# One PSUM bank for two convolution tiles: projections of 256 columns, with the causal tail carried from half to half

## The chip, the cores and the metric

The kernel runs on one core of a Trainium2 chip. Its time is the device time of one execution in microseconds. The core has five engines with instruction queues of their own: TensorE (PE in the profile, its weight loads PEld), VectorE (DVE), ScalarE (ACT), GpSimd (POOL) and SyncE (SP), which here only starts transfers. Matmuls write to PSUM, eight banks of 512 float32 values on each of 128 partitions. Everything here is float32.

## The reference, cut to what matters

The block is a Mamba-2 mixer and a linear layer with sign weights, each behind a modulated layer norm, over 4 sequences of 512 tokens with 512 channels:

```
h    = layernorm(x) * (1 + ca) + sa
proj = h @ in_proj_w.T                   # 2048 channels x|B|C, 1024 z, 64 dt
y    = causal depthwise conv1d(x|B|C, 4 taps)      # pads 3 zeros at the sequence's start
xBC  = silu(y + conv_bias)
...                                      # chunked scan over 128 tokens: decays, C.B, states
out  = ((y_ssm + D * x / dt) * silu(z + z_bias)) @ out_proj_w.T
x    = x + ga * out
x    = x + gb * (sign(W) * mean|W| applied to layernorm(x) * (1 + cb) + sb, + bias)
```

What the change touches is the convolution: output token t takes the projected values of tokens t-3 to t. A token at the start of a stretch needs the three tokens before it.

## The kernel before

The 2048 tokens are worked on in 8 halves of 256 tokens (`T`), two to a sequence (`HPB`); the even half begins a sequence, the odd one continues it. A half has 2 chunks of 128 tokens, and a chunk has 4 units (a group pair `gp` each); so there are 64 units.

**Front of a half.** `f_hT` turns the normed input into `hT`, channels on partitions, with 3 more columns in front: zeros for an even half (a GpSimd memset, L339), the last three columns of the half before for an odd one (a GpSimd copy, L341). `f_dt` makes the step sizes (`pa`, then a series on VectorE). `proj` (L431) multiplies one tile of 128 channels: 4 products over the input channels, which the chip runs as 8 matmul instructions, over all 259 columns for the convolution, over the last 256 for z. So the convolution's values for the three tokens before a half are projected a second time.

`conv_pair` (L436) works on two tiles of 128 channels. Each tile has a PSUM tile `pm` of its own (profile names pp_B, pp_C, pp_x) of 259 columns. ScalarE evicts tap 3 with the bias into `u` (L446), VectorE adds taps 0 to 2 out of PSUM (three multiply-adds, L450), ScalarE takes the tanh of the pair, and VectorE makes the silu (L455). There are 8 pairs in a half: two of B, two of C, four of x. `f_z` does the same for z without a convolution, with two tiles of 256 columns in one PSUM tile (pp_z). `f_Bt` and `f_xt` turn B and x back to tokens on TensorE (pt_bt, pt_xt), and ScalarE copies them out (xpad for x, L489). `f_turned_sums` makes `pn` and `st`.

**PSUM.** `gy` has two banks, `py` one, and all other PSUM tiles share the tag "mm" with five buffers of one bank each:

```python
ps = ctx.enter_context(tc.tile_pool(name="ps", bufs=5, space=PSUM))
```

**A unit.** `stage0` and `stage1` load the running sums, broadcast over partitions, into two of four decay buffers (SyncE's queue), take 16 exponentials of 128x128 on ScalarE (L545), and multiply by C.B on VectorE (L623). `burst` makes the products C.B and C times state (`gy`). `stage2` makes the output `py` in two strips of 16 matmul instructions each (32 columns of the array each, glued together), adds and gates with z on VectorE and GpSimd (L664 to L673), and makes the new state: xd on GpSimd (L680), pst on TensorE (L685), S. `tail1` to `tail3` make the output projection po (L722), the second norm and the linear layer pf (L758) of a chunk.

**Order.** The loop at the end goes through steps, one a unit. In each step, the front's pieces of this step are emitted first, then the burst, `stage2` of the step's unit, and `stage0` and `stage1` of the unit two steps on. The lists FIRST and SECOND (halves 0 and 1) and FRONT (all others) say which piece belongs to which step. FRONT's begin in the half before: step 3 hT and dt, step 4 a B and a C pair, step 5 two x pairs, pn and a turn of B, step 6 a B and a C pair and two turns of x, step 7 two x pairs, steps 8 to 10 z. Half 1 has its first B pair in step 2. Within this, the Tile framework's scheduler orders each engine's instructions when the kernel is built, by program order and by what its cost model takes to be ready; it also gives out the buffers and sets all waits. `tc.issue_after(ins)` keeps instructions of the same engine behind `ins`. Before the change, it holds the first of the py strips for units 4 to 7 alone, behind the last projection of half 1; `behind` does it for turns.

Of the kernel before, what the change touches and what calls it, by code (L numbers as in the profile page):

```python
# [39 lines left out]
def adaln_mamba_block(  # L40
# [26 lines left out]
    keep = ctx.enter_context(tc.tile_pool(name="keep", bufs=1))  # L67
    dram = ctx.enter_context(tc.tile_pool(name="dram", bufs=1, space=bass.MemoryType.DRAM))
    ps = ctx.enter_context(tc.tile_pool(name="ps", bufs=5, space=PSUM))
    wk = ctx.enter_context(tc.tile_pool(name="wk", bufs=2))  # L70
# [43 lines left out]
    win = keep.tile([P, NK, PROJ], F32, name="win")  # L114
# [44 lines left out]
    cw = keep.tile([P, NCONV // P, KS], F32, name="cw")  # L159
    nc.sync.dma_start(cw, conv_w)  # L160
    cb = keep.tile([P, NCONV // P], F32, name="cb")
# [142 lines left out]
    H = [dict(B={}, C={}, xt={}, xs={}, bt={}, z={}) for _ in range(NHALF)]  # L304
# [28 lines left out]

    def f_hT(h, turned=None):
        b = h // HPB

        hT = wk.tile([P, NK, KS - 1 + T], F32, tag="hT", name=f"hT_{h}")
        if h % HPB == 0:
            nc.gpsimd.memset(hT[:, :, 0 : KS - 1], 0.0)  # L339
        else:  # L340
            nc.gpsimd.tensor_copy(hT[:, :, 0 : KS - 1], H[h - 1]["hT"][:, :, T:])  # L341
        for d2 in range(NK // 2):
            pt = turned[d2] if turned else turned_x(h, d2)
            for q in range(2):
                dt = 2 * d2 + q
                nc.scalar.activation(
                    hT[:, dt, KS - 1 :], pt[:, q, :], AF.Identity,
                    bias=modT[:, 0, dt, b : b + 1], scale=modT[:, 1, dt, b : b + 1],
                )
        H[h]["hT"] = hT  # L350

    def f_dt(h):

        hT = H[h]["hT"]

        queue = nc.sync if h == 0 else nc.gpsimd

        def small(tag, bufs=1):
            return wk.tile([P, CH], F32, tag=tag, name=f"{tag}_{h}", bufs=bufs)

        pa = ps.tile([P, CH], F32, tag="mm", name=f"pa_{h}")
        for k in range(NK):
            for c in range(2):
                mm(pa[c * NH : (c + 1) * NH, :], win[:, k, NCONV + DI :],  # L367
                   hT[:, k, KS - 1 + c * CH : KS - 1 + (c + 1) * CH], start=(k == 0), stop=(k == NK - 1))
        u, r, q, dt, relu = (small(n) for n in ("du", "dr", "dq", "da", "dl"))
        nc.vector.tensor_scalar(relu, pa, 0.0, None, ALU.max)  # L370
        nc.scalar.activation(u, pa, AF.Abs)
        nc.scalar.activation(u, u, AF.Exp, scale=-1.0)
        nc.vector.tensor_scalar(r, u, 2.0, None, ALU.add)
        nc.vector.reciprocal(r, r)
        nc.vector.tensor_mul(u, u, r)
        nc.vector.tensor_mul(q, u, u)
        nc.vector.tensor_scalar(dt, q, SERIES[0], None, ALU.mult)
        for cf in SERIES[1:]:
            nc.vector.scalar_tensor_tensor(dt, dt, cf, q, ALU.add, ALU.mult)
        nc.vector.scalar_tensor_tensor(dt, dt, 1.0, u, ALU.add, ALU.mult)  # L380
        nc.vector.scalar_tensor_tensor(dt, dt, 2.0, relu, ALU.mult, ALU.add)

        up = relu
        nc.vector.tensor_tensor_scan(up, ones, dt, 0.0, ALU.mult, ALU.add)
        sh = small("sh", 2)
        nc.vector.tensor_scalar(sh, up, up[:, CH // 2 - 1 : CH // 2], None, ALU.subtract)
        with tc.issue_after(last_win):
            queue.dma_start(sums_d[h].rearrange("c h s -> (c h) s"), sh)
        es = small("es", 2)
        nc.scalar.activation(es, up, AF.Exp, scale=-1.0)  # L390
        with tc.issue_after(last_win):
            queue.dma_start(e_d[h].rearrange("c h s -> (c h) s"), es)

        ntot = wk.tile([P, 1], F32, tag="ntot", name=f"ntot_{h}", bufs=1)
        nc.vector.tensor_scalar(ntot, up[:, CH - 1 : CH], -1.0, None, ALU.mult)
        ed = u
        nc.scalar.activation(ed, up, AF.Exp, bias=ntot)

        dg = q
        nc.vector.tensor_scalar(dg, ident, es[:, CH - 1 : CH], None, ALU.mult)  # L400

        nc.vector.reciprocal(r, dt)
        nc.vector.tensor_scalar(r, r, dsk, None, ALU.mult)
        with tc.issue_after(last_win):
            for c in range(2):
                queue.dma_start(r_d[h, :, c, :], r[c * NH : (c + 1) * NH, :])
        H[h].update(turn=(sh, ed, dg))
# [20 lines left out]
            st=st[:, 0:P], ed=st[:, P : 2 * P], dec=st[:, 2 * P :].rearrange("p (j h) -> p j h", h=HPG)  # L428
        )

    def proj(pm, h, col, lo):  # L431
        for k in range(NK):
            last = mm(pm, win[:, k, col : col + P], H[h]["hT"][:, k, lo:], start=(k == 0), stop=(k == NK - 1))  # L433
        return last.ins

    def conv_pair(h, t0, name, dst=None):  # L436

        u = wk.tile([P, 2, T], F32, tag="u", name=f"u_{name}_{h}", bufs=4)
        for j in range(2):
            t = t0 + j
            pm = ps.tile([P, KS - 1 + T], F32, tag="mm", name=f"pp_{name}{j}_{h}")
            H[h]["last"] = proj(pm, h, t * P, 0)
            nc.scalar.activation(  # L446
                u[:, j, :], pm[:, KS - 1 :], AF.Identity, bias=cb[:, t : t + 1], scale=cw[:, t, KS - 1 : KS]
            )
            for k in range(KS - 1):
                nc.vector.scalar_tensor_tensor(  # L450
                    u[:, j, :], pm[:, k : k + T], cw[:, t, k : k + 1], u[:, j, :], ALU.mult, ALU.add
                )
        th = wk.tile([P, 2, T], F32, tag="th", name=f"th_{name}_{h}")
        nc.scalar.activation(th, u, AF.Tanh)
        nc.vector.scalar_tensor_tensor(u if dst is None else dst, th, 1.0, u, ALU.add, ALU.mult)  # L455
        return u
# [49 lines left out]
    def f_z(h, j):  # L506
        pm = ps.tile([P, 2, T], F32, tag="mm", name=f"pp_z{j}_{h}")
        for q in range(2):
            H[h]["last"] = proj(pm[:, q, :], h, NCONV + (2 * j + q) * P, KS - 1)
        u = wk.tile([P, 2, T], F32, tag="u", name=f"uz_{h}_{j}", bufs=4)  # L510
        for q in range(2):
            nc.scalar.activation(  # L512
                u[:, q, :], pm[:, q, :], AF.Identity, bias=zb[:, 2 * j + q : 2 * j + q + 1], scale=0.5
            )
        th = wk.tile([P, 2, T], F32, tag="th", name=f"thz_{h}_{j}")
        nc.scalar.activation(th, u, AF.Tanh)
        z = wk.tile([P, 2, T], F32, tag="z", name=f"z_{h}_{j}", bufs=6)
        nc.vector.scalar_tensor_tensor(z, th, 1.0, u, ALU.add, ALU.mult)
        H[h]["z"][j] = z
# [108 lines left out]
    def stage2(h, c, gp):  # L628
# [4 lines left out]
        n = f"{h}_{c}_{gp}"  # L633
        k = (h % HPB) * 2 + c
# [12 lines left out]
        for r in range(2):  # L647
            glued([
                partial(
                    mm, py[32 * j : 32 * j + 32, r, :],  # L650
                    xp[:, r * 2 * P + 32 * (2 * j + q) : r * 2 * P + 32 * (2 * j + q) + 32],
                    ets[r][:, 2 * j + q, :], start=(q == 0), stop=(q == 1),
                )
                for q in range(2) for j in range(HPG // 2)
            ], H[1]["last"] if (h, c) == (0, 1) else None)

        cs = slice(c * CH, (c + 1) * CH)
        zg = H[h]["z"][gp][:, :, cs]
# [1 line left out]
        t = wk.tile([P, 2, CH], F32, tag="gm", name=f"yt_{n}", bufs=3)  # L660
# [14 lines left out]
        if k < HPB * 2 - 1:  # L675
# [8 lines left out]
            for r in range(2):  # L684
                mm(pst[r * NS : (r + 1) * NS, :], bt[:, r * NS : (r + 1) * NS], xd2[:, r * P : (r + 1) * P],  # L685
                   start=True, stop=True)
# [77 lines left out]
    def behind(h, f, *args):  # L764
# [9 lines left out]
        (7, f_x, (2,)), (7, behind, (f_Bt, 1)), (7, f_x, (3,)),  # L774
        (8, f_z, (0,)), (8, behind, (f_xt, 2)), (8, f_z, (1,)), (8, behind, (f_xt, 3)),
        (9, f_z, (2,)), (10, f_z, (3,)),
    ]

# [15 lines left out]
    NU = 2 * NP  # L794
    steps = {}

    def at(step, f, *args):
        steps.setdefault(step, []).append((f, args))

    for h in range(NHALF):  # L800
        for step, f, args in (FIRST, SECOND)[h] if h < 2 else FRONT:
            at(max(0, h - 1) * NU + step, f, h, *args)
        if h % HPB == 0:
            at(h * NU + 3, load_gates, h // HPB)
        if h == 0:
            at(0, load_late, h)
            at(1, behind, 0, late_mods)
            at(2, load_wout)
            for o in range(NK):
                at(o // 2 + 2, signs, o)  # L810
# [12 lines left out]
    h = NHALF - 1  # L823
# [65 lines left out]
```

## Time and profile before

| | |
|---|---|
| time, three runs | 748.45 us median (746.47 to 752.62) |
| profiled execution | 747.6 us, of which the span of the profile is 745.9 us |
| mean granted clock of TensorE | 0.991 |
| busy: TensorE, VectorE, ScalarE, GpSimd | 711.2, 602.6, 523.7, 260.4 us |
| matmuls of the convolution (pp_x, pp_B, pp_C) | 512, 256, 256 of 259 columns |
| matmuls of z | 512 of 256 columns |

Busy time counts an engine's instructions from start to end, and matmuls overlap; so the spacing of matmuls in the chain or the timeline says more of their cost than their mean duration. A wait is put down to the instruction that came last among those waited for, as far as the profile tells. A wait of TensorE for an instruction of ScalarE or VectorE can be for data or for a PSUM bank that this instruction was the last to read.

### The profile page before, as it was taken

Reading aid. Unit: us, or ns where it says so; the run is one execution under the profiler, and the core shown is the slowest. Engines: PE = TensorE matmul, PEld = TensorE weight load, DVE = VectorE, ACT = ScalarE, POOL = GpSimd, SP = SyncE. Lnnn points to the kernel's source line nnn. Section 1 sums busy time; section 2 is a strip of 40 time slices with the busy share of each in tenths; the row PEclk is TensorE's granted clock in tenths of the full one; section 3 lists DMA queues with packets and bytes.
Section 4 is the critical chain, followed back from the end, with each engine's and each line's share of the span. In section 5 each row is a group of like instructions: output and inputs, shape, how many; then the busy total and the mean of one; then the engine's idle time right before and its main releaser. Section 6 shows DMA issues by size and latency. Waiting matters only on the chain.

```text
span 745.9 us, 15107 instructions
## 1 busy us (share of the span) xinstructions
PE 711.2 (95%) x5196; PEld 503.2 (67%) x5196; DVE 602.6 (81%) x1218; ACT 523.7 (70%) x1507; POOL 260.4 (35%) x313
## 2 busy tenths in 40 slices
PE   6999979899999999999999999999999999999997
PEld 3787647566677666686667666876667866677654
DVE  3968889866999579986899769996699867997795
ACT  2476668648796596775877777764969658798941
POOL 4021325334242433353224243533324232343452
PEclk9999989899999999999999999999999999999999
DMA  8991865435654266434634246543544436458610
GB/s 280 317 289 39 237 164 121 113 86 138 125 146 125 63 158 140 106 101 99 158 101 119 75 108 165 149 110 69 139 125 121 129 79 175 104 152 167 143 58 28
DMA packets 119068, 99.25 MB, mean 133 GB/s; under 512 B 73984, under 2 KB 97152, under 8 KB 118992
## 3 DMA queue, kind: packets, MB, share of 16 engines
q1 hardware_dynamic: 117808, 96.39, 50.6%
q0 software_dynamic: 896, 1.38, 0.6%
q8 instruction: 41, 0.67, 0.4%
q10 hardware_dynamic: 288, 0.52, 0.2%
q14 instruction: 35, 0.29, 0.1%
HBM read 92.47 MB, written 5.79 MB: 132 GB/s over the span
## 4 chain that ended last, share of the span: by engine, by line
PE 77%; ACT 14%; DVE 5%; issue 2%; DMA 2%; ACTq 0%; POOL 0%; SPq 0%; DVEq 0%
PE pp_x L433 16%; PE po L722 15%; PE pp_z L433 12%; ACT decay L545 10%; PE pp_B L433 7%; PE pp_C L433 7%; PE pf L758 4%; PE py L211 3%; PE py L214 3%; PE gy L211 2%; PE pt_xt L463 2%; PE pst L685 2%; PE pa L367 1%; DMA decay<-sums_d 1%; ACT h L742 1%
## 5 line engine op out<-in xcount | busy, mean ns | idle before, releaser
L545 ACT ACTIVATE decay<-decay,st 128x128 f32<-128x128 f32 x960 | 293.0, 395 | 4.0 <-DMA decay<-sums_d 3.7
L623 DVE SCALAR_TENSOR_TENSOR decay<-decay,gm 128x1024 f32<-128x1024 f32 x120 | 156.8, 1308 | 25.1 <-ACT decay L545 24.1
L433 PE MATMUL pp_x<-hT,win 128*128 128x259 f32 x512 | 122.5, 394 | 5.8 <-ACT decay L545 5.8
L433 PE MATMUL pp_z<-hT,win 128*128 128x256 f32 x512 | 118.1, 383 | 0.0
L433 PEld LDWEIGHTS pp_x<-hT,win 128*128 128x128 f32 x512 | 98.0, 195 | 24.1 <-ACT decay L545 6.0
L722 PE MATMUL po<-wout,z 128*128 128x512 f32 x256 | 113.9, 595 | 0.0
L433 PEld LDWEIGHTS pp_z<-hT,win 128*128 128x128 f32 x512 | 94.3, 189 | 16.1 <-issue 3.3
L680 POOL TENSOR_TENSOR xd<-xpad,st 128x256 f32<-128x256 f32 x48 | 37.6, 784 | 188.3 <-PE pst L685 143.0
L450 DVE SCALAR_TENSOR_TENSOR u_x<-pp_x,cw,u_x 128x256 f32<-128x256 f32 x192 | 82.9, 473 | 1.4 <-ACT u_x L446 0.5
L722 PEld LDWEIGHTS po<-wout,z 128*128 128x128 f32 x256 | 47.4, 190 | 52.6 <-issue 51.7
L512 ACT ACTIVATE uz<-pp_z,zb 128x256 f32<-128x256 f32 x64 | 26.8, 468 | 62.3 <-PE pp_z L433 62.3
L670 POOL TENSOR_TENSOR yt<-yt,xs 128x256 f32<-128x256 f32 x46 | 41.1, 893 | 84.4 <-DVE yt L669 84.4
L214 PE MATMUL py<-decay,xpad 128*32 128x128 f32 x1680 | 67.4, 276 | 0.0
L673 POOL TENSOR_TENSOR z<-yt,z 128x256 f32<-128x256 f32 x62 | 58.5, 944 | 17.1 <-DVE yt L672 13.6
L433 PE MATMUL pp_B<-hT,win 128*128 128x259 f32 x256 | 60.9, 388 | 0.9 <-ACT st L426 0.9
L758 PE MATMUL pf<-bwT,h 128*128 128x512 f32 (+1 forms) x136 | 59.1, 575 | 0.8 <-ACT h L742 0.6
L433 PE MATMUL pp_C<-hT,win 128*128 128x259 f32 x256 | 59.0, 382 | 0.0
L503 POOL TENSOR_TENSOR xs<-u_x,rr 128x512 f32<-128x512 f32 x32 | 42.1, 1318 | 40.8 <-DVE u_x L455 40.8
L433 PEld LDWEIGHTS pp_B<-hT,win 128*128 128x128 f32 x256 | 47.0, 189 | 10.8 <-ACT st L426 1.7
L433 PEld LDWEIGHTS pp_C<-hT,win 128*128 128x128 f32 x256 | 47.8, 189 | 7.8 <-DVE u_B L450 0.3
L446 ACT ACTIVATE u_x<-pp_x,cb,cw 128x256 f32<-128x256 f32 x64 | 35.2, 559 | 25.1 <-PE pp_x L433 24.8
L211 PE MATMUL py<-decay,xpad 128*32 128x128 f32 x240 | 47.5, 280 | 3.8 <-ACT decay L545 2.8
(155 smaller groups left out, 1134.0 us busy)
## 6 DMA issues: line engine op xcount, KB each, us to landing
decay<-sums_d SPq DMA_DIRECT2D x120, 256.0 KB
decay<-sums_d SPq DMA_DIRECT2D x120, 128.0 KB
rr<-r_d SPq DMA_DIRECT2D x64, 128.0 KB
e<-e_d SPq DMA_DIRECT2D x96, 64.0 KB
win<-in_w_inT SPq DMA_DIRECT2D x4, 1024.0 KB
xr<-in_x SPq DMA_DIRECT2D x16, 256.0 KB
res<-o SPq DMA_DIRECT2D x15, 256.0 KB
x<-in_x SPq DMA_DIRECT2D x14, 256.0 KB
```

Source lines behind the costliest of these rows:

```text
L211: first = products[0]()
L214: product()
L433: last = mm(pm, win[:, k, col : col + P], H[h]["hT"][:, k, lo:], start=(k == 0), stop=(k == NK - 1))
L450: nc.vector.scalar_tensor_tensor(u[:, j, :], pm[:, k : k + T], cw[:, t, k : k + 1], u[:, j, :], ALU.mult, ALU.add)
L503: nc.gpsimd.tensor_tensor(xs, xc, rr, ALU.mult)
L545: nc.scalar.activation(ets[r][:, i, :], ets[r][:, i, :], AF.Exp, bias=H[h]["st"][:, hd : hd + 1], scale=-1.0)
L623: nc.vector.scalar_tensor_tensor(ets[r], ets[r], 1.0, bc_mid(gm[:, r, :], HPG), ALU.min, ALU.mult)
L670: ew.tensor_add(t, t, xs)
L673: ew.tensor_mul(zg, t, zg)
L680: nc.gpsimd.tensor_tensor(xd, xg, by_head(H[h]["ed"][:, hd0 : hd0 + HPP]), ALU.mult)
L722: last_po = mm(po, H[h]["z"][g // 2][:, g % 2, c * CH : (c + 1) * CH], wout[:, g, :], start=(g == 0), stop=(g == NKI - 1))
L758: mm(pf, h2[:, k, :], bwT[:, k, cols], start=(k == 0), stop=(k == NK - 1))
```

## The change

`hT` has 256 columns and none in front, and both memset and copy on GpSimd go. A convolution pair's two tiles share one PSUM tile of 2x256 columns, one bank. All projections of the pair are emitted before its evictions. In an even half, ScalarE copies the pair's last three projected columns to `ctail`. `f_carry`, five GpSimd operations in an odd half, makes from `ctail` what taps 0 to 2 of the half before add to the first three tokens; VectorE adds this `carry` to `u`, and the multiply-adds then run over 253 to 255 columns. Where a sequence begins, nothing is added, which is the zero padding. The first py strip of every unit is kept behind the last projection emitted so far (`newest["proj"]`).

```diff
     def f_hT(h, turned=None):
         b = h // HPB
-
-        hT = wk.tile([P, NK, KS - 1 + T], F32, tag="hT", name=f"hT_{h}")
-        if h % HPB == 0:
-            nc.gpsimd.memset(hT[:, :, 0 : KS - 1], 0.0)
-        else:
-            nc.gpsimd.tensor_copy(hT[:, :, 0 : KS - 1], H[h - 1]["hT"][:, :, T:])
+        hT = wk.tile([P, NK, T], F32, tag="hT", name=f"hT_{h}")
...
-    def proj(pm, h, col, lo):
+    def proj(pm, h, col):
         for k in range(NK):
-            last = mm(pm, win[:, k, col : col + P], H[h]["hT"][:, k, lo:], start=(k == 0), stop=(k == NK - 1))
+            last = mm(pm, win[:, k, col : col + P], H[h]["hT"][:, k, :], start=(k == 0), stop=(k == NK - 1))
+        newest["proj"] = last.ins
         return last.ins
...
+    ctail = keep.tile([P, NCONV // P, KS - 1], F32, name="ctail")
+    carry = keep.tile([P, NCONV // P, KS - 1], F32, name="carry")
+    ctmp = keep.tile([P, NCONV // P, KS - 1], F32, name="ctmp")
+
+    def f_carry(h):
+        for k in range(KS - 1):
+            n = KS - 1 - k
+            to = carry if k == 0 else ctmp
+            nc.gpsimd.tensor_tensor(to[:, :, 0:n], ctail[:, :, k:], bc(cw[:, :, k], n), ALU.mult)
+            if k > 0:
+                nc.gpsimd.tensor_add(carry[:, :, 0:n], carry[:, :, 0:n], ctmp[:, :, 0:n])
+
     def conv_pair(h, t0, name, dst=None):
...
+        both = slice(t0, t0 + 2)
         u = wk.tile([P, 2, T], F32, tag="u", name=f"u_{name}_{h}", bufs=4)
+        pm = ps.tile([P, 2, T], F32, tag="mm", name=f"pp_{name}_{h}")
+        for j in range(2):
+            H[h]["last"] = proj(pm[:, j, :], h, (t0 + j) * P)
         for j in range(2):
             t = t0 + j
-            pm = ps.tile([P, KS - 1 + T], F32, tag="mm", name=f"pp_{name}{j}_{h}")
-            H[h]["last"] = proj(pm, h, t * P, 0)
             nc.scalar.activation(
-                u[:, j, :], pm[:, KS - 1 :], AF.Identity, bias=cb[:, t : t + 1], scale=cw[:, t, KS - 1 : KS]
+                u[:, j, :], pm[:, j, :], AF.Identity, bias=cb[:, t : t + 1], scale=cw[:, t, KS - 1 : KS]
             )
+        if h % HPB < HPB - 1:
+            nc.scalar.copy(ctail[:, both, :], pm[:, :, T - KS + 1 :])
+        if h % HPB:
+            nc.vector.tensor_add(u[:, :, 0 : KS - 1], u[:, :, 0 : KS - 1], carry[:, both, :])
+        for j in range(2):
+            t = t0 + j
             for k in range(KS - 1):
+
+                past = KS - 1 - k
+                uk = u[:, j, past:]
                 nc.vector.scalar_tensor_tensor(
-                    u[:, j, :], pm[:, k : k + T], cw[:, t, k : k + 1], u[:, j, :], ALU.mult, ALU.add
+                    uk, pm[:, j, 0 : T - past], cw[:, t, k : k + 1], uk, ALU.mult, ALU.add
                 )
...
-            ], H[1]["last"] if (h, c) == (0, 1) else None)
+            ], newest["proj"])
...
+    for h in range(1, NHALF, 2):
+        at((h - 1) * NU + 2, f_carry, h)
```

More of the change, by code (lines that the diff above doesn't have):

```diff
@@ L346, in f_hT @@
                 nc.scalar.activation(
-                    hT[:, dt, KS - 1 :], pt[:, q, :], AF.Identity,
+                    hT[:, dt, :], pt[:, q, :], AF.Identity,
                     bias=modT[:, 0, dt, b : b + 1], scale=modT[:, 1, dt, b : b + 1],
@@ L367, in f_dt @@
                 mm(pa[c * NH : (c + 1) * NH, :], win[:, k, NCONV + DI :],
-                   hT[:, k, KS - 1 + c * CH : KS - 1 + (c + 1) * CH], start=(k == 0), stop=(k == NK - 1))
+                   hT[:, k, c * CH : (c + 1) * CH], start=(k == 0), stop=(k == NK - 1))
         u, r, q, dt, relu = (small(n) for n in ("du", "dr", "dq", "da", "dl"))
@@ L429, in f_turned_sums @@
         )
-    def proj(pm, h, col, lo):
+    def proj(pm, h, col):
         for k in range(NK):
-            last = mm(pm, win[:, k, col : col + P], H[h]["hT"][:, k, lo:], start=(k == 0), stop=(k == NK - 1))
+            last = mm(pm, win[:, k, col : col + P], H[h]["hT"][:, k, :], start=(k == 0), stop=(k == NK - 1))
+        newest["proj"] = last.ins
         return last.ins
+    newest = {}
+    ctail = keep.tile([P, NCONV // P, KS - 1], F32, name="ctail")
[8 more added lines that the diff above has]
+                nc.gpsimd.tensor_add(carry[:, :, 0:n], carry[:, :, 0:n], ctmp[:, :, 0:n])
     def conv_pair(h, t0, name, dst=None):
+        both = slice(t0, t0 + 2)
         u = wk.tile([P, 2, T], F32, tag="u", name=f"u_{name}_{h}", bufs=4)
+        pm = ps.tile([P, 2, T], F32, tag="mm", name=f"pp_{name}_{h}")
+        for j in range(2):
+            H[h]["last"] = proj(pm[:, j, :], h, (t0 + j) * P)
         for j in range(2):
             t = t0 + j
-            pm = ps.tile([P, KS - 1 + T], F32, tag="mm", name=f"pp_{name}{j}_{h}")
-            H[h]["last"] = proj(pm, h, t * P, 0)
             nc.scalar.activation(
-                u[:, j, :], pm[:, KS - 1 :], AF.Identity, bias=cb[:, t : t + 1], scale=cw[:, t, KS - 1 : KS]
+                u[:, j, :], pm[:, j, :], AF.Identity, bias=cb[:, t : t + 1], scale=cw[:, t, KS - 1 : KS]
             )
+        if h % HPB < HPB - 1:
[4 more added lines that the diff above has]
+            t = t0 + j
             for k in range(KS - 1):
+                past = KS - 1 - k
+                uk = u[:, j, past:]
                 nc.vector.scalar_tensor_tensor(
-                    u[:, j, :], pm[:, k : k + T], cw[:, t, k : k + 1], u[:, j, :], ALU.mult, ALU.add
+                    uk, pm[:, j, 0 : T - past], cw[:, t, k : k + 1], uk, ALU.mult, ALU.add
                 )
@@ L508, in f_z @@
         for q in range(2):
-            H[h]["last"] = proj(pm[:, q, :], h, NCONV + (2 * j + q) * P, KS - 1)
+            H[h]["last"] = proj(pm[:, q, :], h, NCONV + (2 * j + q) * P)
         u = wk.tile([P, 2, T], F32, tag="u", name=f"uz_{h}_{j}", bufs=4)
```

## The prediction

> **What bounds the kernel now.** I read the page first: the engines' busy times, the slices, the chain that ended last.
>
> ```profile
> PE 711.2 (95%) x5196; PEld 503.2 (67%) x5196; DVE 602.6 (81%) x1218; ACT 523.7 (70%) x1507; POOL 260.4 (35%) x313
> ...
> PE   6999979899999999999999999999999999999997
> ...
> PEclk9999989899999999999999999999999999999999
> ...
> PE 77%; ACT 14%; DVE 5%; issue 2%; DMA 2%; ACTq 0%; POOL 0%; SPq 0%; DVEq 0%
> ```
>
> TensorE is busy 95% of the span and makes 77% of the chain; the weak slices, and the two with a lower clock, lie in the first fifth. Next came the chain in order of time (start, length, work), for the pace of the projections.
>
> ```profile
> 92.64 0.84 DVE dr L402
> 96.62 1.56 ACT decay L545 x5
> 98.30 5.44 PE pp_x L433 x16
> ...
> 134.31 6.18 PE pp_x L433 x16
> 140.92 3.51 PE pp_x L433 x16
> ...
> 190.96 3.51 PE pp_C L433 x16
> ...
> 240.68 3.46 PE pp_z L433 x16
> ```
>
> Sixteen matmuls of 259 columns take 3.51 us, sixteen of 256 columns (pp_z) 3.46 us. Two groups stand out with 5.44 and 6.18 us, each behind a pause. Stretches around these and one steady half (length, busy time of the engines, then granted clock) show what happens there.
>
> ```profile
> 92.30:98.30 6.00, 0.23 (x5) 0.03 (x1) 6.00 (x16) 4.16 (x12) 3.08 (x5) 0.72 1.08 255
> 98.30:103.70 5.40, 5.40 (x18) 4.41 (x18) 5.40 (x13) 4.58 (x14) 1.09 (x2) 0.68 1.04 238
> 130.20:133.60 3.40, 0.21 (x4) 0.04 (x3) 1.38 (x3) 3.40 (x11) 3.32 (x5) 0.84 0.76 189
> 134.20:140.80 6.60, 6.60 (x23) 5.32 (x22) 6.43 (x12) 4.72 (x15) 2.37 (x3) 0.61 0.71 190
> 187.20:273.40 86.20, 84.95 (x625) 61.00 (x623) 71.96 (x146) 64.20 (x187) 29.19 (x36) 1.00 0.47 115
> ```
>
> In the first pause VectorE is busy all 6.00 us, in the second ScalarE all 3.40 us, and the clock is low afterwards. In a steady half of 86.2 us TensorE has hardly a gap, VectorE has 14.2 us free. Last, TensorE's waits, up to 150 us (the first three lines) and after.
>
> ```profile
> PE pp_x L433 <- ACT decay L545: 5.8, 1, 5.8
> PE pst L685 <- ACT xpad L489: 3.2, 1, 3.2
> PE ph L740 <- ACT decay L545: 1.4, 1, 1.4
> ...
> PE pt_bt L463 <- ACT decay L545: 1.1, 3, 0.4
> PE pp_B L433 <- ACT st L426: 0.9, 3, 0.3
> PE pt_xt L463 <- DVE u_B L450: 0.9, 1, 0.9
> PE ph L740 <- ACT st L426: 0.5, 3, 0.2
> ```
>
> The engines named don't make these tiles' inputs: they are readers that give a bank back. At 92 us the five banks of the tag "mm" hold two C tiles, two x tiles and pst, and the next x tile waits for VectorE's third multiply-add on the first C tile (98.1 us). At 297.6 us four x tiles and pn fill all five, and pt_bt waits.
>
> [...]
>
> **The change part by part.** The sum is made against the profiled execution, 747.6 us (span 745.9 and 1.7 around it), 0.85 below the median of 748.45.
>
> Width. 8 halves x 16 tiles x 8 matmuls = 1024 matmuls lose three columns: 0.05 us / 16 = 3.1 ns each, 3.2 us. Nearly all lie on the path: -3.2.
>
> Banks, steady part. A pair of conv tiles takes one bank in place of two. With two x pairs, pn, pt_bt and ph there are five tiles for five banks, so the waits of 1.1, 0.9, 0.9 and 0.5 us (3.4) should go. What is late next there is TensorE's own work; I take -3.0. The waits of pa for hT and of py for the decays are for data and stay.
>
> Banks, first pause. With pairs, C, x0, pst and x1 need four banks, so x1 can start at 92.6. In reach are 5.8 us and the cold clock, 5.44 - 3.51 = 1.9, together 7.7. Late next is VectorE (busy 6.00 of 6.00, then 5.40 of 5.40 us), and behind it the output product po, which needs z that GpSimd wrote only at 102.4 to 103.2, one us before po began. So between 1.4 and 7.7; VectorE's order also moves: -4.5.
>
> Banks, second pause. ScalarE's sixteen exponentials stand ahead of the readers of every bank, and one bank gained lets pst pass, not the x pair behind it. Of 3.2 + (6.18 - 3.51) us and of ph's 1.4 I take -1.5; bounds 0 and -7.3.
>
> Later start of a pair. The first eviction waits for the second tile, 8 x 0.22 = 1.75 us more. In the steady part each pair is used steps later and hides it. In the first half, x0's turn at 34 us already waits 1.5 us for its multiply-adds: +1.7 there, 0 if VectorE gets to its dt series sooner.
>
> Tail copies. 4 halves x 8 pairs = 32 ScalarE copies of 128x6; the nearest row is a 128x16 activation, 0.22 us: 7.0 us. ScalarE is 14% of the chain: +1.0. Between 0 and 7.0.
>
> Carry adds. 32 VectorE adds of 128x6 at 0.15 us (the row of 128x4) are 4.9 us; the 384 multiply-adds lose one to three columns, near 2 ns each, -0.8. VectorE is 5% of the chain: +0.2; between 0 and 4.1.
>
> GpSimd. Eight small memsets and copies go (1.4 us); f_carry's five operations in four halves come, 20 at 0.2 (copy) to 0.78 us (multiplication of 128x128), 4 to 16 us. GpSimd is busy 29.2 of 86.2 us, and f_carry stands two steps, some 21 us, ahead of its use: 0. If it sat behind a state product that waits for TensorE (up to 10.4 us once), the cover would still hold. In the second half the use is in the same step; there up to +2.
>
> Strips behind the projections. In the trace every unit's py already follows its step's projections, but one: unit 2 (75.3 us) runs ahead of the second half's B pair. Moved behind it, its wait of 1.1 us goes and about 1.0 us of work no longer fills TensorE's wait for hT: 0. Behind it are queued its pst and the loads into the two decay buffers that it frees (SyncE's queue), some 4 us later, for unit 4 at 112 us, over 25 us on.
>
> Sum: -3.2 - 3.0 - 4.5 - 1.5 + 1.7 + 1.0 + 0.2 = -9.3: 738.3 for the profiled execution, 739.1 for a median. I say 739.0.
>
> **Rivals.**
> A: only the width pays. The start is bound by VectorE and ScalarE together (VectorE 86% busy from 50 to 134 us), so the pauses come back elsewhere, and pairs that read later cost what the steady waits gave: -3.2, 745.3. For it speaks 6.00 of 6.00; against it that the steady waits have no other engine behind them.
> B: both pauses close. -3.2 - 3.4 - 7.7 - 7.3 + 1.5 = -20: 728. Against it, GpSimd's z and ScalarE's unbroken 3.40 us.
> C, the slow side: VectorE becomes the bound. Its multiply-adds wait in its queue for the two evictions and the tail copy, with ScalarE's groups of eight exponentials (2.43 us) between. A steady half has 14.2 us free and eight pairs, so up to 1.75 us of waiting per pair is free. At 2.1 us it costs 8 x 2.1 - 14.2 = 2.6 us in each of six steady halves, with the adds 17: about 762 less 3.2, 759. Against it: before, the multiply-adds waited for evictions 1.8 us in all.
>
> **How the numbers follow.** Forecast 0.49 (own range 732 to 744), A 0.27, B 0.11, C 0.13. The range of 727 to 753 leaves out most of C and the far end of B. A measurement here tells about 1%, 7.5 us, from no change: faster takes B and 0.42 of the forecast, 0.53; same A and the rest, 0.36; slower most of C, 0.11.
>
> **What would show it.** Right: pp_x, pp_B and pp_C at 3.46 us a pair; no pause near 92 us, a clock near 1 behind it; no waits of pt_bt and pp_B for readers. Right on cost: the tail copy near 0.2 us, VectorE's busy time some 4 us up. Wrong: waits of VectorE for the evictions above 1.75 us a pair (C), or TensorE's idle time up to 150 us unchanged under other names (A).

## The result and the profile after

The changed kernel takes 766.88 us (median of four runs, 765.81 to 768.69) against 747.6 us for four runs of the kernel before beside it: 1.0246 times as long, 95% interval 1.0215 to 1.0276. The prediction was 739.0 us, faster. Among the variants below, one execution of no_carry ran in a slower state at a lower clock (776.45 us at 0.94, the others at 0.984 to 0.992), and its time and ratio are those of the other three. The profiled execution took 767.4 us with a span of 765.5 us, 19.6 us more than the 745.9 us of before. These lines of its page answer to those shown of before:

```profile
PE 716.1 (94%) x5196; PEld 508.3 (66%) x5196; DVE 614.2 (80%) x1250; ACT 522.5 (68%) x1539; POOL 272.0 (36%) x325
...
PE   6898978999998999999999899999999899999997
...
PEclk9999988999999999999999999999999999999999
```

Nothing stands out here: TensorE is 4.9 us busier, in a span 19.6 us longer, and the slices are too coarse. So I took the start of the first B projection of each half as a mark. The third half begins at 187.2 us before and at 191.6 after: 4.4 us lost at the start. The lengths from there, half by half, are 86.2, 90.5, 86.2, 89.5, 86.2 before and 90.6, 90.3, 90.8, 89.6, 90.8 after: the three even ones lose 4.4, 4.6 and 4.6 us, the two odd ones next to nothing (-0.2 and +0.1). From the last mark to the end it is 120.2 and 121.8, 1.7 us more. The sum is 19.6 us.

The stretches of the third to fifth half (length, busy time of PE, PEld, DVE, ACT, POOL, then the granted clock) show TensorE idle 4.4 us in an even half, where it was 1.25 us before, and a granted clock of 0.98:

```profile
191.60:282.20 90.60, 86.22 (x623) 62.24 (x622) 73.62 (x146) 65.19 (x199) 31.38 (x40) 0.98 0.44 110
282.20:372.50 90.30, 87.25 (x656) 62.41 (x655) 76.12 (x160) 63.58 (x185) 35.46 (x40) 1.00 0.46 120
372.50:463.30 90.80, 86.32 (x625) 62.24 (x623) 74.00 (x146) 65.57 (x199) 31.81 (x40) 0.98 0.47 111
```

TensorE's waits after 150 us (total, times, longest) name it. The largest is new, the turn of an x pair (`f_xt`, back to tokens) waiting for that pair's SiLU:

```profile
PE pt_xt L487 <- DVE u_x L479: 12.6, 11, 2.4
PE py L211 <- ACT decay L569: 3.2, 4, 0.9
PE pst L709 <- ACT st L421: 3.0, 3, 1.0
PE pp_B L428 <- ACT st L421: 1.4, 2, 0.8
PE ph L764 <- DVE t L299: 1.1, 3, 0.4
```

The long one, 2.4 us, comes once in each even half, and there it is the turn of x2, the third of the four x pairs (x0 to x3). These are that pair's rows in the third half of the kernel before, from its timeline (start, length, engine, and in brackets the idle time ahead; other rows are left out):

```profile
229.99 3.15 DVE L450 SCALAR_TENSOR_TENSOR u_x<-pp_x,cw,u_x 128x256 f32<-128x256 f32 x6
231.02 0.56 ACT L446 ACTIVATE u_x<-pp_x,cb,cw 128x256 f32<-128x256 f32 x1 [1.13 <-PE pp_x L433]
234.30 0.62 ACT L454 ACTIVATE th_x<-u_x 128x512 f32<-128x512 f32 x1
235.58 0.68 DVE L455 SCALAR_TENSOR_TENSOR u_x<-th_x,u_x 128x512 f32<-128x512 f32 x1
...
240.08 0.60 PE L463 MATMUL pt_xt<-ident,u_x 128*128 128x128 f32 x4
```

VectorE's multiply-adds begin at 229.99, before the second tile is even evicted. The pair's last projection ends at 231.0. The SiLU is done at 236.3 and the turn begins at 240.1: 3.8 us of slack. The same pair in the changed kernel:

```profile
231.69 3.72 PE L428 MATMUL pp_x<-hT,win 128*128 128x256 f32 x16
...
235.51 1.02 ACT L461 ACTIVATE u_x<-pp_x,cb,cw 128x256 f32<-128x256 f32 x2 [1.00 <-PE pp_x L428]
236.43 0.98 ACT L569 ACTIVATE decay<-decay,st 128x128 f32<-128x128 f32 x3
237.30 0.62 ACT L478 ACTIVATE th_C<-u_C 128x512 f32<-128x512 f32 x1
237.82 1.56 ACT L569 ACTIVATE decay<-decay,st 128x128 f32<-128x128 f32 x5
239.28 0.15 ACT L465 COPY ctail<-pp_x 128x6 f32<-128x6 f32 x1
240.74 0.47 DVE L474 SCALAR_TENSOR_TENSOR u_x<-pp_x,cw,u_x 128x253 f32<-128x253 f32 x1
...
246.83 0.69 DVE L479 SCALAR_TENSOR_TENSOR u_x<-th_x,u_x 128x512 f32<-128x512 f32 x1
247.57 0.66 PE L487 MATMUL pt_xt<-ident,u_x 128*128 128x128 f32 x4 [2.39 <-DVE u_x L479]
248.07 5.31 PE L428 MATMUL pp_z<-hT,win 128*128 128x256 f32 x16
```

Both evictions come behind both projections: the last one ends at 235.4 us, and they begin at 235.51. The tail copy, the last read of the bank by ScalarE, stands behind eight exponentials and a tanh and ends 4.0 us after the last projection (235.4). VectorE, which has two other products ahead in its queue, turns to the pair at 240.74, 5.3 us after the last projection, and the SiLU ends 12.1 us after it, where it was 5.3. The turn waits 2.4 us. Then the matmuls of z run at half clock: the granted clock is 0.50 from 248.4 to 251.8 us, and this row takes 5.31 us, against 3.72 us for the same row at full clock (241.04 us). 2.4 and 1.6 are 4.0 of the 4.4 us.

### The profile page after: what moved, and what is told of

Its sections match the earlier page's. It is cut to its first block, busy times and chain, and to the rows that moved or that the text cites. A ratio compares the mean times of both kernels' runs of the same rounds, so it can differ in the third digit from the quotient of the medians.

```text
span 765.5 us, 15156 instructions
## 1 busy us (share of the span) xinstructions
PE 716.1 (94%) x5196; PEld 508.3 (66%) x5196; DVE 614.2 (80%) x1250; ACT 522.5 (68%) x1539; POOL 272.0 (36%) x325
## 3 DMA queue, kind: packets, MB, share of 16 engines
q0 software_dynamic: 896, 1.38, 0.6%
## 5 line engine op out<-in xcount | busy, mean ns | idle before, releaser
L647 DVE SCALAR_TENSOR_TENSOR decay<-decay,gm 128x1024 f32<-128x1024 f32 x120 | 153.5, 1281 | 27.0 <-ACT decay L569 21.4
L428 PE MATMUL pp_z<-hT,win 128*128 128x256 f32 x512 | 125.1, 400 | 0.0
L428 PE MATMUL pp_x<-hT,win 128*128 128x256 f32 x512 | 116.7, 382 | 0.0
L428 PEld LDWEIGHTS pp_z<-hT,win 128*128 128x128 f32 x512 | 99.5, 199 | 17.6 <-issue 3.9
L428 PEld LDWEIGHTS pp_x<-hT,win 128*128 128x128 f32 x512 | 95.2, 190 | 14.9 <-issue 2.8
L704 POOL TENSOR_TENSOR xd<-xpad,st 128x256 f32<-128x256 f32 x48 | 34.6, 721 | 177.4 <-PE pst L709 137.6
L474 DVE SCALAR_TENSOR_TENSOR u_x<-pp_x,cw,u_x 128x253 f32<-128x253 f32 (+2 forms) x192 | 85.0, 471 | 0.8 <-ACT ctail L465 0.3
L527 POOL TENSOR_TENSOR xs<-u_x,rr 128x512 f32<-128x512 f32 x32 | 50.7, 1585 | 44.0 <-DVE u_x L479 43.4
L428 PE MATMUL pp_C<-hT,win 128*128 128x256 f32 x256 | 61.1, 393 | 2.7 <-DVE u_B L474 2.3
L428 PE MATMUL pp_B<-hT,win 128*128 128x256 f32 x256 | 60.2, 386 | 1.4 <-ACT st L421 1.4
L428 PEld LDWEIGHTS pp_B<-hT,win 128*128 128x128 f32 x256 | 47.1, 190 | 10.3 <-ACT st L421 1.9
```

The lines of the kernel that those rows point to most:

```text
L428: last = mm(pm, win[:, k, col : col + P], H[h]["hT"][:, k, :], start=(k == 0), stop=(k == NK - 1))
L474: nc.vector.scalar_tensor_tensor(uk, pm[:, j, 0 : T - past], cw[:, t, k : k + 1], uk, ALU.mult, ALU.add)
L527: nc.gpsimd.tensor_tensor(xs, xc, rr, ALU.mult)
L647: nc.vector.scalar_tensor_tensor(ets[r], ets[r], 1.0, bc_mid(gm[:, r, :], HPG), ALU.min, ALU.mult)
L704: nc.gpsimd.tensor_tensor(xd, xg, by_head(H[h]["ed"][:, hd0 : hd0 + HPP]), ALU.mult)
```

## The experiments

All runs in one table: ratio to the kernel before with its interval, and from the profiled execution, in us, the start of the third half, the mean of the even halves (the 3rd, 5th and 7th) and of the odd ones (the 4th and 6th), and the last stretch. The four stretches come from one execution each. The times of one kernel's executions lie 2 to 8 us apart (old_strips and no_carry: over 6 us), so a start that differs by a few us can be scatter.

| kernel | ratio (95%) | third half | even | odd | last |
|---|---|---|---|---|---|
| before | 1 | 187.2 | 86.2 | 90.0 | 120.2 |
| after | 1.0246 (1.0215 to 1.0276) | 191.6 | 90.7 | 89.9 | 121.8 |
| tail_last | 1.0239 (1.0203 to 1.0274) | 191.7 | 90.4 | 90.4 | 121.8 |
| two_banks | 1.0049 (1.0030 to 1.0068) | 191.0 | 86.3 | 90.1 | 121.4 |
| old_strips | 1.0096 (1.0064 to 1.0128) | 190.4 | 88.8 | 89.4 | 123.3 |
| turn_late | 1.0183 (1.0161 to 1.0205) | 191.0 | 88.4 | 90.0 | 123.3 |
| two_banks_old_strips | 1.0093 (1.0065 to 1.0121) | 191.9 | 86.4 | 90.2 | 121.4 |
| before_strips | 0.9982 (0.9972 to 0.9993) | 187.0 | 86.2 | 90.3 | 120.2 |
| pair_order | 1.0194 (1.0164 to 1.0224) | 188.2 | 87.1 | 92.2 | 124.2 |
| no_carry | 1.0167 (1.0123 to 1.0210) | 192.0 | 89.7 | 89.8 | 120.6 |
| reads_first | 1.0136 (1.0114 to 1.0158) | 195.3 | 87.3 | 89.0 | 121.0 |
| reads_first_turn_late | 1.0074 (1.0054 to 1.0094) | 197.3 | 86.4 | 88.5 | 120.4 |
| two_banks_no_carry | 1.0020 (1.0010 to 1.0030) | 188.6 | 86.4 | 89.7 | 121.1 |
| first_batch_before | 0.9969 (0.9957 to 0.9980) | 187.1 | 86.4 | 88.5 | 120.4 |

**tail_last.** The tail copy behind the multiply-adds.

```diff
-        if h % HPB < HPB - 1:
-            nc.scalar.copy(ctail[:, both, :], pm[:, :, T - KS + 1 :])
...
                     uk, pm[:, j, 0 : T - past], cw[:, t, k : k + 1], uk, ALU.mult, ALU.add
                 )
+        if h % HPB < HPB - 1:
+            nc.scalar.copy(ctail[:, both, :], pm[:, :, T - KS + 1 :])
```

> The changed kernel with ScalarE's tail copy put behind the pair's six multiply-adds, so that they wait for the two evictions alone. Theory T1 (the tail copy sits in ScalarE's queue behind exponentials and holds VectorE's multiply-adds up, in even halves only): even halves fall from 90.6 back to about 86 us, three times -4.5, about 753 us. Theory T2 (two tiles in one bank: the multiply-adds wait for the second tile's matmuls and eviction, in all halves): the delay from the last matmul to the first multiply-add falls from 5.2 to no less than 4 us, the time stays above 760. Theory T3 (the strips' new place): no change, 766.

766.16 us: nothing changed, so the tail copy as such isn't the cause. ScalarE's timeline for x2 says why. The pair's second eviction has taken the copy's place behind the exponentials, and the delay is the same:

```profile
236.33 0.56 ACT L461 ACTIVATE u_x<-pp_x,cb,cw 128x256 f32<-128x256 f32 x1 [2.71 <-PE pp_x L428]
237.00 0.16 ACT L476 COPY ctail<-pp_C 128x6 f32<-128x6 f32 x1
237.06 0.63 ACT L478 ACTIVATE th_C<-u_C 128x512 f32<-128x512 f32 x1
237.59 2.43 ACT L569 ACTIVATE decay<-decay,st 128x128 f32<-128x128 f32 x8
239.93 0.55 ACT L461 ACTIVATE u_x<-pp_x,cb,cw 128x256 f32<-128x256 f32 x1
```

So the theory became: VectorE waits for ScalarE's last read of the shared bank, whichever it is.

**two_banks.** A bank for each tile again, each tile evicted behind its own projection; 256 columns, carry and strips stay.

```diff
-        pm = ps.tile([P, 2, T], F32, tag="mm", name=f"pp_{name}_{h}")
         for j in range(2):
+            pm = ps.tile([P, T], F32, tag="mm", name=f"pp_{name}{j}_{h}")
-            H[h]["last"] = proj(pm[:, j, :], h, (t0 + j) * P)
+            H[h]["last"] = proj(pm, h, (t0 + j) * P)
...
```

> The changed kernel with a PSUM bank for each tile again (256 columns), each tile's eviction, tail copy, carry and multiply-adds straight behind its own projection; carry and strips stay. T2: the delay to the first multiply-add is back at 1 to 2 us, the turn of x no longer waits, 742 to 748 us. T1: the tail copy still stands ahead of the multiply-adds, even halves stay near 90 us, above 757. T3: no change, 766.

751.82 us, above the 742 to 748 expected for it. The even halves are back at 86.3 us, and the SiLU of x2 ends 5.4 us after the last projection. Sharing a bank and the emission order that goes with it cost together some 15 us of the 19. The waits of the kernel before for a free bank are back too, 2.8 us at pt_bt and 2.2 at pp_B.

**old_strips.** The changed kernel with the old hold on the strips.

```diff
-            ], newest["proj"])
+            ], H[1]["last"] if (h, c) == (0, 1) else None)
```

> The changed kernel with the old hold of the py strips (units 4 to 7 behind half 1's last projection, no other). T3: most of the 19 us come back, below 755. T1 and T2: 763 to 768; at most the 4 us of the start move.

757.62 us, between the two expectations and with a wide spread (753.18 to 760.83): the strips cost some 9 us in this kernel. The profiled execution was the slowest of the five, so its timeline shows only part of it. In the third half, without the hold behind the newest projection, a unit's strips now stand ahead of x2's turn and fill 1.1 us of its wait; the rest is 1.38 us, the next sixteen matmuls take 3.62 us, the pace of full clock, and the third half takes 86.0 us:

```profile
244.22 0.30 PE L211 MATMUL py<-decay,xpad 128*32 128x128 f32 x1
...
246.68 0.66 PE L487 MATMUL pt_xt<-ident,u_x 128*128 128x128 f32 x4 [1.38 <-DVE u_x L479]
247.17 3.62 PE L428 MATMUL pp_z<-hT,win 128*128 128x256 f32 x16
```

In the fifth and seventh half it is these strips that wait, 1.9 us each time, and slow matmuls follow: sixteen of z take 4.11 and 5.24 us there. The two halves take 90.1 and 90.5 us, hardly less than in the changed kernel:

```profile
424.27 0.27 PE L211 MATMUL py<-decay,xpad 128*32 128x128 f32 x1 [1.90 <-ACT th_x L478]
...
603.95 0.27 PE L211 MATMUL py<-decay,xpad 128*32 128x128 f32 x1 [1.89 <-ACT th_x L478]
```

**before_strips and two_banks_old_strips.** The strips alone, in the kernel before; and two_banks without them.

```diff
...
-            ], H[1]["last"] if (h, c) == (0, 1) else None)
+            ], newest["proj"])
```

> The kernel before with nothing of the change but the strips: the first py strip of every unit behind the last projection emitted. If the strips' hold costs by itself: 752 to 757, from the first two halves on, since there unit 2 moves. If, as the prediction had it, every other unit follows its projections anyway: within 2 us of 748.

> A bank for each tile again and the old hold of the strips: of the change only the 256 columns and the carry stay. If sharing the bank and the strips make up the whole loss: below the kernel before by about the 3 us of the narrower matmuls, 743 to 747. If the strips only cost where the banks are shared: 752, as with separate banks alone. If the carry itself costs: above 750, with the loss at the start.

746.74 and 754.56 us. Alone the strips cost nothing (0.9982), and with separate banks they even save about 3 us by the medians, though the two intervals touch. What is left of the loss in two_banks_old_strips lies at the start (191.9). So the strips hurt only together with the shared bank and its order: in the third half because the turn of x2 has no slack left and a strip could have filled its wait. Where the rest of the 9 us lies isn't shown.

**turn_late.** x2's turn behind the second pair of z.

```diff
-        (8, f_z, (0,)), (8, behind, (f_xt, 2)), (8, f_z, (1,)), (8, behind, (f_xt, 3)),
+        (8, f_z, (0,)), (8, f_z, (1,)), (8, behind, (f_xt, 2)), (8, behind, (f_xt, 3)),
```

> The changed kernel with the turn of the third x pair put behind the second z pair (3.5 us of matmuls) of its step, where TensorE waits 2.6 us for VectorE in even halves. If that wait and the slow clock behind it are what the even halves lose: three times -4.4, about 753 us, with pp_z at 3.46 us again. If VectorE is the bound and the wait only shows there: it turns up at the next reader of VectorE's work, above 761.

762.37 us, where 753 was expected: even halves 88.4. The mean granted clock of the profiled execution is 0.988, in the changed kernel 0.982, and about half of the even halves' loss is gone, but waits at the turns remain (7.3 us after 191 us, the longest 1.7), as the other expectation said, which took VectorE for the bound.

**pair_order.** A bank for each tile, but both projections emitted first, as in the change.

```diff
-        pm = ps.tile([P, 2, T], F32, tag="mm", name=f"pp_{name}_{h}")
+        pms = [ps.tile([P, T], F32, tag="mm", name=f"pp_{name}{j}_{h}") for j in range(2)]
...
```

> The changed kernel with a PSUM bank for each tile, but everything still emitted in the changed order: both projections first, then the two evictions, the tail copies, the carry, the six multiply-adds. If it is the shared bank [...]: the first eviction comes before the second tile's matmuls end, the delay from the last matmul to the first multiply-add is near 1 to 2 us, the time near 752. If it is the order of emission that places the multiply-adds late in VectorE's queue: the delay stays near 5 us and the time above 760.

761.57 us, above the 760 that stood for the order. Averaged over the pairs from the third half on, the multiply-adds begin 2.4 us after the last projection instead of 5.0. But for x2 in the even halves, the pair that decides, it is 6.1 to 6.3 us, more than the 5.3 of the changed kernel. ScalarE's rows for it in the third half, then VectorE's:

```profile
234.01 0.55 ACT L461 ACTIVATE u_x<-pp_x,cb,cw 128x256 f32<-128x256 f32 x1
234.46 2.44 ACT L570 ACTIVATE decay<-decay,st 128x128 f32<-128x128 f32 x8
236.80 0.55 ACT L461 ACTIVATE u_x<-pp_x,cb,cw 128x256 f32<-128x256 f32 x1
```

```profile
236.93 1.23 DVE L648 SCALAR_TENSOR_TENSOR decay<-decay,gm 128x1024 f32<-128x1024 f32 x1 [0.96 <-ACT decay L570]
238.07 3.20 DVE L475 SCALAR_TENSOR_TENSOR u_x<-pp_x,cw,u_x 128x253 f32<-128x253 f32 x8
```

Each tile has a bank of its own, and still eight exponentials stand between the two evictions, and VectorE comes to the pair behind a decay product that waits for them. So emitting both projections ahead of both evictions is enough to make x2 late; the shared bank isn't needed for it. What the bank adds isn't separated: here the turn waits only 0.3 us and the even halves take 87.1 us, but the odd halves take 92.2 us, 2.2 more than before, by my reading because each pair holds two banks for longer.

**no_carry.** The changed kernel without the tail copies, the products on GpSimd and the adds; the odd halves lack the taps from the half before.

```diff
-        if h % HPB < HPB - 1:
-            nc.scalar.copy(ctail[:, both, :], pm[:, :, T - KS + 1 :])
-        if h % HPB:
-            nc.vector.tensor_add(u[:, :, 0 : KS - 1], u[:, :, 0 : KS - 1], carry[:, both, :])
...
-    for h in range(1, NHALF, 2):
-        at((h - 1) * NU + 2, f_carry, h)
```

> The changed kernel without tail copies, f_carry and carry adds: the odd halves' first three tokens lack the taps of the half before. If the carry's own instructions cost (ScalarE's copies and GpSimd's and VectorE's waits): 755 or less. If not: 763 to 767, with even halves at 90 us as before.

Three executions took 756.68 to 763.04 us, between the two expectations; by the ratios the carry accounts for about 6 of the 19 us. The third half still begins at 192.0 us and two even halves take 89.8 and 91.2: again exponentials between the two evictions.

**reads_first.** Both evictions and the tail copy with a priority, so that nothing gets between them.

```diff
-        for j in range(2):
...
+        with tc.high_priority(offset=1000):
+            for j in range(2):
+                t = t0 + j
+                nc.scalar.activation(
...
+            if h % HPB < HPB - 1:
+                nc.scalar.copy(ctail[:, both, :], pm[:, :, T - KS + 1 :])
```

> The changed kernel with one edit: the two evictions of a pair and its tail copy carry a high priority, so that ScalarE takes them one behind the other and no group of eight exponentials stands between two reads of the shared bank. Theory 1 (the loss of the even halves is the multiply-adds' wait for ScalarE's last read of a shared bank, held up by exponentials): from the last matmul of x2 to its SiLU 12.3 us becomes at most 10, the turn of x2 finds its rows, the 2.5 us waits at 245, 426 and 606 us and the slow clock behind them go, the halves h2, h4, h6 take 86 to 87.5 us instead of 90.7, and the time is 752 to 757 us. Theory 2 (it is the sharing itself: VectorE starts on the pair only when both projections and both evictions are over, wherever the exponentials stand): the even halves stay at 89.5 to 91 us and the time at 762 to 768 us.

The median is 758.55 us, between the two theories; the halves decide. ScalarE's timeline, then VectorE's, show the three reads together and VectorE, idle for 0.57 us until the tail copy ends, on the pair at once, 1.2 us after the last projection:

```profile
239.47 1.02 ACT L462 ACTIVATE u_x<-pp_x,cb,cw 128x256 f32<-128x256 f32 x2 [0.52 <-PE pp_x L428]
240.38 0.16 ACT L466 COPY ctail<-pp_x 128x6 f32<-128x6 f32 x1
240.42 2.45 ACT L570 ACTIVATE decay<-decay,st 128x128 f32<-128x128 f32 x8
...
244.32 2.45 ACT L570 ACTIVATE decay<-decay,st 128x128 f32<-128x128 f32 x8
246.66 0.62 ACT L479 ACTIVATE th_x<-u_x 128x512 f32<-128x512 f32 x1
```

```profile
240.57 2.42 DVE L475 SCALAR_TENSOR_TENSOR u_x<-pp_x,cw,u_x 128x253 f32<-128x253 f32 x5 [0.57 <-ACT ctail L466]
```

The even halves take 87.3 us, the wait at the turn is 0.8 us at most, and the granted clock is 1.00 in the third and in the fourth half. So keeping the exponentials out from between the pair's reads gives back three quarters of the even halves' loss. Whether they delay VectorE through the shared bank or through the order of its queue, this run doesn't tell. The delay itself is not gone: the SiLU of x2 ends 9.8 us after the last projection, where it was 12.1 and, before the change, 5.3. The multiply-adds end 5.2 us after it instead of 2.2, and the tanh stands behind a second group of exponentials. The third half now begins 3.7 us later still, at 195.3.

**reads_first_turn_late.** The priority and the late turn together.

> The same priority, and x2's turn moved behind the second pair of z as well, which gives VectorE some 7 us more. Theory 1: little is left to win by it, halves of 86 to 87.5 us as without the move, 751 to 757 us. Theory 2: like the move alone, 760 to 763 us, even halves of 88 us. If both causes add (the exponentials are one part of the delay, the sharing the other), it is the lower of the two by 2 us or more, and the waits at the turn of x2 are under 0.5 us each.

753.88 us, 4.7 us below the priority alone: the third case of the expectation, that both causes add. The turns' waits in the steady part are gone. The even halves are within 0.2 us of before (86.2), the odd ones 1.5 us shorter on average, and TensorE is busy 84.19 us in an even half against 84.95:

```profile
197.30:283.70 86.40, 84.19 (x625) 61.26 (x623) 73.34 (x146) 63.99 (x195) 32.00 (x40) 1.00 0.48 115
283.70:372.20 88.50, 86.65 (x656) 62.58 (x655) 75.21 (x160) 65.43 (x191) 33.77 (x40) 1.00 0.51 124
372.20:458.60 86.40, 84.19 (x625) 61.27 (x623) 73.32 (x146) 63.39 (x193) 31.98 (x40) 1.00 0.49 114
```

The five halves take 436.2 us; before 438.5. Nearly all that is lost, 10.1 us, lies ahead of 197.3 us.

**two_banks_no_carry.** two_banks without the carry (left out as in no_carry), to ask about the start.

> A bank for each tile and projections of 256 columns, but the carry left out: no tail copies, no product on GpSimd, no adds (the odd halves lack the taps that reach into the half before). It asks where the 3 to 4 us at the start come from that all kernels with the changed convolution have ahead of the third half (191 us there, 187.2 in the kernel before). If the carry's instructions make them: the third half begins at 187 to 188 us and the time is 745 to 748 us, the width of 256 columns paying 1 to 3 us. If it is the order in which the scheduler now takes the instructions at the start, whatever the carry: 190 to 192 us and 749 to 753 us.

749.48 us, so with separate banks the carry costs some 2 us. The third half begins at 188.6 us, against 191.0 with the carry, between what the two sides expected. But pair_order with the carry begins at 188.2 and no_carry, with shared banks, at 192.0. No single part explains the start.

**first_batch_before.** The first two halves with the convolution of the kernel before (`conv_wide`: 259 columns, a bank for each tile); the rest as in reads_first_turn_late.

```diff
+    def conv_wide(h, t0, name, dst):
...
     def conv_pair(h, t0, name, dst=None):
+        if h < HPB:
+            return conv_wide(h, t0, name, dst)
...
+    i = FRONT.index((8, f_z, (1,)))
+    FRONT[i - 1 : i + 1] = FRONT[i], FRONT[i - 1]
```

> The candidate, put together from the runs: the first batch (halves 0 and 1) keeps the convolution of the kernel before, with 259 columns and a bank for each tile; the halves from the third on have the changed one, with the priority for the reads of the shared bank and x2's turn behind the second pair of z; the strips stand behind the newest projections. Theory: the loss at the start is of the changed convolution in the first two halves, so the third half begins at 187 to 189 us again, and the steady halves take 86.4 and 88.5 us as they did with the priority and the late turn (kernel before: 86.2 and 89.5 to 90.5); 743 to 746 us, 0.994 to 0.998 of the kernel before. Rival: the start is late for another reason (the new orders of the whole program move it), the third half begins at 191 us or later, and the time is 747 to 751 us.

746.53 us, half a us above the range expected, and 0.9969 of before (0.9957 to 0.9980). The third half begins at 187.1 us; the halves behind it take what they took with the priority and the late turn (86.4 and 88.5). It is faster than both kernels, by 0.3% than the kernel before, and by its interval isn't told apart from before_strips, which has nothing of the change but the strips.

## Why the prediction was wrong

**Later start of a pair: the step that failed.** I put it at 1.75 us, counted it in one place of the first half, and wrote "In the steady part each pair is used steps later and hides it." That is false for x2, whose turn had 3.8 us of slack and no more, a number the timeline of before would have given me. And the delay was not 1.75 us. The SiLU of x2 ends 6.8 us later after the last projection, 12.1 us instead of 5.3. With the reads kept together it is 9.8, so 2.3 us go with the exponentials between the reads, and 4.5 us remain, which alone are more than the slack. In these 4.5 is the first eviction, which starts 1.75 us later, as I had it: that it comes behind the second tile was an assumption then, and the rows of the changed kernel show it (235.51 us, 0.1 behind the last projection). The rest, later multiply-adds and tanh, isn't taken apart. Averaged over all pairs from the third half on, the multiply-adds begin 5.0 us after the last projection instead of 0.9. ScalarE's last read ends at 3.1 instead of 1.4, so it explains 1.7 of these 4.1 us; the rest is VectorE coming to the pair later. The even halves lost 13.6 us; reads_first gives 10.3 of these back, with the late turn 13.0.

**The clock, left out.** I read the low clock in the first pauses and had no new wait to price with it. The wait of 2.4 us cost another 1.6 us behind it (5.31 us instead of 3.72), and each of the three even halves has such a wait (2.39, 2.44 and 2.44 us) and 3.4 us at a granted clock of 0.50.

**Rival C had the place and not the form.** It named the wait of the multiply-adds for the last read behind eight exponentials, but made VectorE the bound of each steady half, with 1.75 us a pair free. VectorE is no bound (73.6 of 90.6 us busy); one turn with little slack decides. Its 759 us with 0.13 was the nearest, and by its own terms it is 762: 748.45 and 17, less 3.2, which my 759 takes off a second time. Its counter-argument, that the multiply-adds waited only 1.8 us before, was about a kernel with separate banks.

**First and second pause** (-4.5 and -1.5, and +1.7 for x0): instead the start lost 4.4 us. The pause at 92 us went, and the time came back later as other waits up to 192 us:

```profile
PE pt_bt L487 <- ACT st L421: 3.3, 1, 3.3
PE pt_xt L487 <- DVE u_x L479: 3.3, 3, 1.3
PE pp_C L428 <- DVE u_B L474: 2.3, 1, 2.3
PE pm L245 <- DVE rows L242: 2.2, 1, 2.2
```

In the stretch up to the third half TensorE is idle 22.9 us (191.60 less 168.67), before 20.9 (187.20 less 166.32), and busy 2.35 us more. The granted clock falls to 0.50 in three places there, at 74.3, 105.0 and 128.9 us, for 3.4, 6.8 and 6.8 us, each time during a wait of 2.2 to 3.3 us or within 1.4 us behind it; before, it did so in two, at 94.9 and 132.5 us, for 6.8 us each. I had named VectorE as late next and still booked a gain. Why VectorE and ScalarE are later there stays open: the variants begin the third half between 187.0 and 197.3 us, and the carry, the banks and the strips don't order them. Shown is only that with the old convolution in the first two halves it begins at 187.1 again.

**Banks, steady part** (-3.0) **and width** (-3.2): the waits for a bank at pt_bt, at pt_xt behind u_B and at ph behind st (2.5 us) are gone in the changed kernel. But by the same reading others came in their place, all for a bank that ScalarE's copy to st gives back: pst waits 3.0 us and pp_B 1.4 instead of 0.9. That is 4.4 us against 3.4, and 5.9 with the reads kept together and the late turn. So waits for banks moved and didn't go. The gain in the five halves, 2.3 us with the reads together and the late turn, is less than half of what the two steps promise (five eighths of the width's 3.2, and the 3.0), and about what the width alone would give; in the changed kernel itself the odd halves stayed at 90.

**Tail copies, adds, GpSimd.** The rows by line and form:

```profile
L465 ACT COPY ctail<-pp_x 128x6 f32<-128x6 f32 x16 | 2.5, 154 | 0.0
L444 POOL TENSOR_TENSOR carry<-ctail,cw 128x48 f32<-128x48 f32 x4 | 1.8, 448 | 12.4 <-ACT ctail L465 12.4
L446 POOL TENSOR_TENSOR carry<-carry,ctmp 128x32 f32<-128x32 f32 x4 | 1.0, 260 | 0.3
```

A copy takes 0.15 us, not 0.22, and no wait of VectorE for GpSimd's `carry` shows. The copies' busy time was right and small. VectorE's was not: it rose by 11.6 us, where I had named some 4, and the multiply-adds are 4.2 us of it (170.2 to 174.4), which I had 0.8 us shorter. no_carry puts the carry at about 6 us in the changed kernel, and with separate banks it is some 2, against the 1.2 I took and an upper end of 11.1. In x2 of the changed kernel the cost is where the copy stands, but without it a second eviction stands there (tail_last).

**Strips.** 0 is right for the kernel before (0.9982). It is wrong for the changed one: costed alone, it left out that two parts of a change can use up the same slack. That is shown for the third half of old_strips and argued for the rest.

## What to carry to other kernels

Before two tiles share a PSUM bank, list who reads it and on which engine. Here VectorE stood idle for 0.57 us until ScalarE's tail copy ended, whose result the multiply-adds don't use (reads_first), and eight exponentials and a tanh between ScalarE's reads went with a SiLU 12.1 us behind the last projection, against 9.8 without them between. Emitting two tiles' projections ahead of their evictions made the pair late with a bank each as well: its multiply-adds began 6.1 to 6.3 us after the last projection (pair_order). Then look for the consumer with the least slack, read in the timeline as the gap from producer's end to consumer's start (3.8 us for x2's turn before the change), rather than for the engine with the most work. And if the bank is shared, keep the reads together: here one priority gave back 10 of 13.6 us in the steady part, while the start came 3.7 us later.

## What was unexpected of the hardware

Behind a wait of 2.4 us at TensorE the clock fell to half: the granted clock is 0.50 from 248.4 to 251.8 us, 3.4 us, which cost 1.6 us of matmul time. In old_strips the matmuls behind waits of 1.9 us were slow too (sixteen of z in 4.11 and 5.24 us). But the length of a wait alone doesn't decide. In no_carry a wait of 3.3 us left the clock full, as the pace of the matmuls behind it shows (3.62 us for sixteen):

```profile
426.31 0.66 PE L483 MATMUL pt_xt<-ident,u_x 128*128 128x128 f32 x4 [3.29 <-DVE u_x L475]
426.81 3.62 PE L428 MATMUL pp_z<-hT,win 128*128 128x256 f32 x16
```

In the traces of the two kernels, before and after, all changes of clock within the span lie whole steps of 3.41 us apart: the slow stretches last 6.83 us, twice, before the change, and 3.41 us four times and 6.83 us twice after it, each during a wait of 2.2 to 5.8 us or within 1.4 us behind it. What decides whether a wait is followed by one isn't shown.
